# Perceiver kernel, one core: where the last values, the maximum, the NaN check and layer 3's preparations stand

## Chip, cores, metric

The kernel runs on one core of one Trainium2 chip. The metric is the device time of one execution in microseconds; 3083.25 is the median of three runs (3079.7 to 3084.26).

## What is computed

Four layers; each adds to x (128 tokens of width 256) a cross-attention over a context of 12544 tokens of width 192, then a self-attention over the 128 tokens, then a mixture of experts. The cross-attention of layers 0 to 2 has 16 heads of 16; layer 1 is its fullest form:

```python
q = (query @ Wq + bq).reshape(B, Nq, H, D).transpose(0, 2, 1, 3)
k = (key_value @ Wk + bk).reshape(B, Nkv, H, D).transpose(0, 2, 1, 3)
v = (key_value @ Wv + bv).reshape(B, Nkv, H, D).transpose(0, 2, 1, 3)
attn = jnp.einsum('bhqd,bhkd->bhqk', q, k) * scale
attn = jnp.clip(attn, -CLAMP, CLAMP)
attn = jax.nn.softmax(attn, axis=-1)
attn = jnp.where(jnp.any(jnp.isnan(attn)), jnp.asarray(1.0 / Nkv, attn.dtype), attn)
x = jnp.einsum('bhqk,bhkd->bqhd', attn, v).reshape(B, Nq, Cq)
return x @ Wo + bo
```

Layer 0 has no bias and a key mask; layer 2 has biases and neither clip nor NaN test. Layer 3 has 16 heads of 64, key and value weights with a low-rank addition (`down @ up * alpha / RANK`), and a second attention over the last four context tokens with weights of its own (`Wk_ipa`, `Wv_ipa`).

## The kernel before

A planner orders the instructions: each has a rank by its place in the program, and an engine takes the first by rank that the planner's model holds ready. So work that is written later can fill the gaps of what is written earlier: in the timeline, keys of layer 1 (tile `kv`, L102) run from 557 us on, within layer 0's self-attention, though they are written behind layer 0's experts. Each engine then runs its instructions in the order so found. `in_order` (L224) fixes the written order for some stretches.

`attend_twice_in` (L510) is the cross-attention of layers 0 to 2. For each group g of 8 heads it goes over the context's 25 blocks of 512 tokens (the last has 256) twice. In the first sweep, `highest` (L543) makes scores on TensorE (L551, with mask rows from L550 in layer 0) into one of four PSUM pairs (tile `pair`), and VectorE takes their maximum per query, head and block (`parts`, L552). Each block has four such calls: s in 0, 1 and two halves. Between them `keys.project` (L152) makes the keys and values of blocks further on, up to block 21; the keys of blocks 22 to 24 too, but not their values. `add_up` (L94) sums the context on POOL in layer 1. When the sweep is over, `project_values` (L171) makes the values of blocks 22 and 23, then of 24, on TensorE (recorded at L102), and ScalarE copies them (L136). Then come the products of `between`, if there is one, and `lowered` (L554): the maximum over blocks, negated, split into three bfloat16 parts, two transposes (L569), and a copy `m` in twice the needed width (L571). `spread` (L574) makes `less` from it (L581); layer 1 makes two `floor` tiles instead (L695). The second sweep makes the scores less the maximum (L585, L592), their exponentials (L636, L651, or L292 and L612 in layer 1), and multiplies with the values (L658).

`between` is the hook by which layer 3's preparations run there. In layer 0, `prepare_l3` (L1049) loads layer 3's key and value weights in block 3 of the first sweep, and adds the low-rank part after the sweep: four 128x512 products for the keys at the end of group 0's sweep and four for the values at the end of group 1's, each pair of products with an addition on VectorE. In layer 2, `last_tokens_l3` (L1093) loads `Wk_ipa`, makes the keys of the last four tokens after group 0's sweep, loads `Wv_ipa` into the same buffer, and makes their values after group 1's.

In layer 1, `nan_guard` (L1015) stands behind both groups: keys and queries are summed up in such a way that a NaN or infinity in them shows, and if one does, `copy_predicated` (L1012) puts the mean of the values in the place of the output `o`, before the output's projection (`project_out`, L462; its transposes are recorded at L450).

The first eight blocks' keys of the next layer (`keys.early`) are made in the self-attention and expert stages in the single PSUM pair `kv` (`early_pair`). Expert weights go through a pool of buffers of one megabyte (`large_weights`; ten in layers 0 and 2, four in 1 and 3). Their DMAs, like most, are issued by SP's queue in order; those of early context blocks by POOL's.

Of the kernel before, what the change touches and what calls it, by code (L numbers as in the profile page):

```python
# [21 lines left out]
P = 128  # L22
D = 256
# [182 lines left out]
class Net:  # L206
# [289 lines left out]
    def attend_twice(self, o, qz, keys, masked=False, clip=None, between=None):  # L496

        self.psum(ppr=4)
        with self.tc.tile_pool(name="twice", bufs=2, reuse_waits="tile") as pool:
            keys.lay(pool)
            self.attend_twice_in(pool, o, qz, keys, masked, clip, between)
        self.singles_and_early()

    def attend_twice_in(self, pool, o, qz, keys, masked, clip, between):  # L510
# [43 lines left out]
        def lowered(parts):  # L554
# [6 lines left out]
            short = self.sp.tile([P, 2, 4], BF16, tag="short", name="short")  # L561
            for j in range(2):
                nc.vector.tensor_copy(short, neg)
                nc.vector.tensor_copy(wide[:, :, :, j], short)
                self.tt(neg, neg, wide[:, :, :, j], ALU.subtract)
            nc.vector.tensor_copy(wide[:, :, :, 2], neg)
# [3 lines left out]
            m = pool.tile([P, 2, HB], BF16, tag="low", name="low", bufs=1)  # L570
            nc.vector.tensor_copy(m, bc(p[:, 0, :HB], 1, 2))  # L571
            return m.rearrange("p c n -> p (c n)")

        def spread(m, half):  # L574

            x = self.pair()
            for i in range(2):
                r = tiles[2 * half + i]
                nc.tensor.matmul(x[:, i, :HB], self.ones16[r, :], m[r, :HB], start=True, stop=True)
            less = pool.tile([P, 2, HB], F32, tag="less", name="less", bufs=1)  # L580
            nc.vector.tensor_copy(less, x[:, :, :HB])  # L581
            return less

        def less_maximum(t, x, m):
            nc.tensor.matmul(x, self.ones16[tiles[t], :], m[tiles[t], :], start=True, stop=False, skip_group_check=True)  # L585
# [30 lines left out]
        def weights(g, c, m, less, row):  # L616
# [8 lines left out]
            else:  # L625
                for j in range(2):
                    at = slice(j * HB, (j + 1) * HB)
                    k = slice((c % 4 + j) * P, (c % 4 + j + 1) * P)
                    for t in range(2):
                        r = tiles[t]  # L630
                        nc.tensor.matmul(x[t][:, at], row[r, k], m[r, at], start=j == 0, stop=False, skip_group_check=True)
# [31 lines left out]
        for g in range(2):  # L663
# [6 lines left out]
            for b in range(NSB):  # L670
# [7 lines left out]
                if between is not None and g == 0 and b == 3:  # L678
                    between[0]()

            keys.project_values(g, [NSB - 3, NSB - 2])
            keys.project_values(g, [NSB - 1])
            if between is not None:
                between[1][g][0](self.pair)
            m = lowered(parts)
            if between is not None:
                between[1][g][1]()
            floor = None
            if clip is not None:
                floor = []  # L690
                for half in range(2):
                    x = self.pair()
                    for i in range(2):
                        r = tiles[2 * half + i]
                        nc.tensor.matmul(x[:, i, :], self.ones16[r, :], m[r, :], start=True, stop=True)  # L695
                    floor.append(pool.tile([P, 2, SB], F32, tag=f"floor{half}", name="floor", bufs=1))
                    self.ts(floor[half], x, -clip, None, ALU.add)
# [38 lines left out]
            oT = pool.tile([P, 2, P], F32, tag="low" if clip is None else "oT", name="oT", bufs=1)  # L736
# [213 lines left out]
    def l0_xattn(self, x):  # L950
        nc, d = self.nc, self.d
        with self.tc.tile_pool(name="x0", bufs=2, reuse_waits="tile") as pool:
# [15 lines left out]
            with self.tc.tile_pool(name="layer3", bufs=1, reuse_waits="tile") as other:  # L968
                self.attend_twice(o, qz, keys, masked=True, between=self.prepare_l3(other))
# [15 lines left out]
    def xattn_biased(self, x, name, guarded, keys):  # L985
        nc, d = self.nc, self.d
        with self.tc.tile_pool(name=name, bufs=2, reuse_waits="tile") as pool:
# [13 lines left out]
            if guarded:  # L1001
                self.attend_twice(o, qz, keys, clip=CLAMP)
            else:
                with self.tc.tile_pool(name="layer3", bufs=1, reuse_waits="tile") as other:
                    self.attend_twice(o, qz, keys, between=self.last_tokens_l3(other))

            self.tt(o, o, bv, ALU.add)
            if guarded:
                bk = self.load_row(d[f"{name}_bk"], D)
                with self.tc.tile_pool(name="guard", bufs=1, reuse_waits="tile") as own:  # L1010
                    bad, mean = self.nan_guard(own, keys.sums, xT, wq, bq, keys.wk, keys.wv, bk, bv)
                    nc.vector.copy_predicated(o, bad.bitcast(U32), mean)  # L1012
            return self.project_out(x, o, wo, [(self.ones[:1, :], bo)])

    def nan_guard(self, pool, totals, xT, wq, bq, wk, wv, bk, bv):  # L1015
# [4 lines left out]
        sums = self.stat(2)  # L1020
        nc.vector.tensor_reduce(sums[:, 0:1], totals[:, :SB], AX.X, ALU.add)
        nc.vector.tensor_reduce(sums[:, 1:2], totals[:, SB:], AX.X, ALU.add)
        wide = pool.tile([P, 2, P], F32, tag="wide", name="wide", bufs=1)
        nc.vector.tensor_copy(wide, bc(sums, 2, P))
        many = pool.tile([1, P], F32, tag="many", name="many", bufs=1)
        nc.vector.memset(many, float(S2))
        p = self.ps()
        self.mm(p[:, :D], [(xT[:, k, :], wq[:, k, :]) for k in range(2)] + [(self.ones[:1, :], bq)])
        q = pool.tile([P, D], F32, tag="gq", name="gq", bufs=1)
        nc.vector.tensor_copy(q, p[:, :D])  # L1030
        p = self.ps()
        self.mm(p[:, :D], [(wide[:, k, :], wk[:, k, :]) for k in range(2)] + [(many, bk)])
        self.tt(q, q, p[:, :D], ALU.mult)
        self.tt(q, q, q, ALU.not_equal)
        found = self.stat(1)
        nc.vector.tensor_reduce(found, q, AX.X, ALU.max)
        p = self.ps()
        self.mm(p[:, :1], [(self.ones, found)])
# [794 lines left out]
```

## Time and profile before

One execution was profiled: 3080.96 us, of which the profile's span is 3079.3 us; its mean granted TensorE clock was 0.966. Stages, read from the timeline, with the busy time in each:

| Stage | from, to (us) | PE | DVE | ACT |
|---|---|---|---|---|
| Layer 0: self-attention and experts | 556 to 685 | 99.2 | 59.1 | 31.2 |
| Layer 1: cross-attention, NaN check | 685 to 1224 | 525.1 | 474.6 | 256.7 |
| Layer 1: output, self-attention | 1224 to 1290 | 55.2 | 44.2 | 22.5 |
| Layer 2: cross-attention | 1361 to 1877 | 506.0 | 364.0 | 243.8 |
| Layer 2: self-attention | 1877 to 1914 | 31.5 | 22.6 | 12.5 |
| Layer 2: experts | 1914 to 1977 | 51.4 | 29.1 | 17.8 |

The six first sweeps of layers 0 to 2 end (last L552) at 163.3, 431.3, 814.1, 1081.6, 1489.7 and 1751.4 us. The busy time of a matmul is a modelled duration and overlaps with its neighbours', so a stage that shows PE busy may still have room in it. In the lines of the profile, `L102` is a helper for keys and values, `L278` and `L289` to `L298` are helpers for matmuls and VectorE operations of many places: there the tile's name says what is meant. A matmul in float32 appears as two records.

### The profile page before, as it was taken

The page shows a single profiled execution, that of the slowest core. Times are in us where ns is not written, and L with a number is a line of the kernel's source. Part 1 is how long each engine was busy: PE and PEld are TensorE (multiplying, and loading weights), DVE is VectorE, ACT ScalarE, POOL GpSimd, SP SyncE. Part 2 cuts the span into 40 slices and gives each one's busy share as a digit, 9 for nine tenths or more (in the row PEclk, how much of TensorE's full clock was granted, in tenths as well). Part 3 has the DMA queues.
Part 4 walks back from the last instruction along what each step waited for, and adds up shares of the span by engine and source line. Part 5 has one row for each costly group of instructions (what it writes and reads, how often), then busy time and mean ns, then how long its engine had stood idle before and what let it go on. Part 6 is the DMA issues. An engine that isn't in the chain of part 4 may idle for free.

```text
span 3079.3 us, 78420 instructions
## 1 busy us (share of the span) xinstructions
PE 2923.5 (95%) x34877; PEld 2212.8 (72%) x34877; DVE 2249.7 (73%) x2887; ACT 1428.3 (46%) x1673; POOL 456.7 (15%) x501
## 2 busy tenths in 40 slices
PE   8999999879999999899999998899999999999979
PEld 5667667535576576675676576489889889889858
DVE  6876877638997897769658755477777777777854
ACT  1167128411383176311482295356556555656521
POOL 6666577212000000120000001000000000000000
PEclk9989999989999998999899999899999999999979
DMA  4200210552002101442102106332322222222436
GB/s 128 60 18 22 70 47 4 190 203 60 27 3 58 55 18 39 135 155 57 31 9 72 50 3 216 109 93 80 85 85 82 85 80 85 85 82 85 123 113 205
DMA packets 166858, 246.96 MB, mean 80 GB/s; under 512 B 21261, under 2 KB 108431, under 8 KB 166520
## 3 DMA queue, kind: packets, MB, share of 16 engines
q1 hardware_dynamic: 160200, 227.67, 24.3%
q0 software_dynamic: 6208, 14.27, 1.5%
q8 instruction: 274, 4.49, 0.6%
q14 instruction: 64, 0.52, 0.1%
q10 hardware_dynamic: 112, 0.01, 0.0%
HBM read 241.75 MB, written 0.13 MB: 79 GB/s over the span
## 4 chain that ended last, share of the span: by engine, by line
PE 79%; DVE 14%; issue 2%; ACT 2%; DMA 2%; POOL 1%; SPq 0%; DVEq 0%; ACTq 0%; POOLq 0%
PE pair L102 20%; PE pair L551 10%; PE acc L658 8%; PE v L102 7%; PE sc L790 6%; PE acc L832 5%; PE pair L592 4%; PE ps L278 4%; PE one L592 4%; DVE parts L552 3%; DVE e L292 2%; PE kv L102 2%; PE acc L278 2%; PE pair L585 2%; PE ps L1624 1%
## 5 line engine op out<-in xcount | busy, mean ns | idle before, releaser
L552 DVE TENSOR_REDUCE parts<-pair 128x2 f32<-128x1024 f32 x600 | 679.3, 1197 | 108.2 <-PE pair L551 108.0
L102 PE MATMUL pair<-ctxA,wk 128*128 128x256 f32 x1236 | 329.7, 400 | 1.4 <-ACT kT L193 1.1
L102 PEld LDWEIGHTS pair<-ctxA,wk 128*128 128x128 f32 x1236 | 217.5, 190 | 140.8 <-DVE parts L552 95.2
L551 PE MATMUL pair<-kT,qz 32*128 32x512 f32 (+1 forms) x1632 | 278.6, 617 | 9.1 <-DVE parts L552 8.9
L289 DVE TENSOR_TENSOR top<-top,kept 128x1024 f32<-128x1024 f32 (+2 forms) x145 | 169.1, 1169 | 133.8 <-ACT kept L792 132.5
L792 ACT COPY kept<-sc 128x1024 f32<-128x1024 f32 (+1 forms) x135 | 136.3, 1010 | 261.1 <-PE sc L790 261.1
L636 ACT ACTIVATE e<-pair 128x1024 f32<-128x1024 f32 x196 | 200.7, 1024 | 82.5 <-PE pair L592 62.1
L292 DVE SCALAR_TENSOR_TENSOR e<-pair,floor 128x1024 f32<-128x1024 f32 x196 | 230.5, 1219 | 6.5 <-PE pair L592 0.4
L612 ACT ACTIVATE e<-e 128x1024 f32<-128x1024 f32 x196 | 206.6, 1057 | 33.7 <-DVE e L292 26.5
L592 PE MATMUL pair<-qz,kT 32*128 32x256 f32 x2112 | 219.0, 374 | 0.0
L536 POOL TENSOR_SCALAR row<-mask 128x512 bf16<-128x512 uint8 (+1 forms) x100 | 189.6, 1896 | 173.7 <-PE pair L551 102.5
L658 PE MATMUL acc<-e,v 128*17 128x128 f32 x6336 | 211.4, 274 | 3.1 <-ACT e L651 2.2
L132 ACT ACTIVATE kT<-pair,bk 128x512 f32<-128x512 f32 (+1 forms) x68 | 45.9, 674 | 348.2 <-PE pair L102 348.2
L292 DVE SCALAR_TENSOR_TENSOR e<-one,maskcol,less 128x256 f32<-128x256 f32 x392 | 162.6, 477 | 58.4 <-PE one L592 41.7
L651 ACT ACTIVATE e<-e 128x1024 f32<-128x1024 f32 x196 | 205.1, 1048 | 0.0
L658 PEld LDWEIGHTS acc<-e,v 128*17 128x17 f32 x6336 | 155.8, 97 | 67.9 <-ACT e L651 45.6
L790 PE MATMUL sc<-qz,kT 64*128 64x128 f32 x2816 | 197.8, 279 | 0.0
L102 PEld LDWEIGHTS v<-wv,ctxA 128*128 128x128 f32 x1568 | 189.8, 192 | 6.4 <-issue 1.7
L102 PE MATMUL v<-wv,ctxA 128*128 128x128 f32 x1568 | 193.1, 276 | 0.0
L289 DVE TENSOR_TENSOR e<-one,less 128x512 f32<-128x512 f32 x196 | 126.4, 686 | 88.8 <-PE pair L592 87.6
L102 PE MATMUL pair<-ctxB,wk 64*128 64x256 f32 x1236 | 188.9, 399 | 0.0
L790 PEld LDWEIGHTS sc<-qz,kT 64*128 64x128 f32 x2816 | 171.6, 187 | 13.0 <-issue 1.3
(439 smaller groups left out, 5495.2 us busy)
## 6 DMA issues: line engine op xcount, KB each, us to landing
ctxA<-in_ctxA SPq DMA_DIRECT2D x324, 256.0 KB
ctxB<-in_ctxB SPq DMA_DIRECT2D x339, 128.0 KB
w<-in_L_ffn_W SPq DMA_DIRECT2D x32, 1024.0 KB
ctxA<-in_ctxA POOLq DMA_DIRECT2D x36, 256.0 KB, 3.1
w<-in_L_ffn_w_gateT SPq DMA_DIRECT2D x8, 1024.0 KB
wu<-in_L_ffn_w_upT SPq DMA_DIRECT2D x8, 1024.0 KB
w<-in_L_ffn_w_downT SPq DMA_DIRECT2D x8, 1024.0 KB
w<-in_L_ffn_w1T SPq DMA_DIRECT2D x8, 1024.0 KB
```

Source lines behind the costliest of these rows:

```text
L102: self.nc.tensor.matmul(out, a, b, start=start and not low, stop=low == 1, skip_group_check=True)
L289: self.nc.vector.tensor_tensor(out, a, b, op)
L292: self.nc.vector.scalar_tensor_tensor(out, a, s, b, op0, op1, **kw)
L536: nc.gpsimd.tensor_scalar(row[:, :n], to[:, :n], 0.0, 1.0, ALU.is_gt, ALU.subtract)
L551: nc.tensor.matmul(x[:, i, :n], qz[r, g, s, :], keys.kT(b)[r, :n], start=not masked, stop=True)
L552: nc.vector.tensor_reduce(parts[:, s, 2 * half : 2 * half + 2, b], x[:, :, :n], AX.X, ALU.max)
L592: nc.tensor.matmul(at, keys.kT(c // 4)[tiles[t], k], q, start=start, stop=True, skip_group_check=True)
L612: nc.scalar.activation(to, to, AF.Exp)
L636: nc.scalar.activation(to, pair, AF.Exp)
L651: nc.scalar.activation(to, to, AF.Exp)
L658: nc.tensor.matmul(acc[32 * t : 32 * t + 17, half, :], v[:, c % 4 + j, 4 * half + t, :], es[half][:, t // 2, j, t % 2, :], start=c + j + h ...
L790: nc.tensor.matmul(x[:, t, c : c + P], kT[r, c : c + P], qz[r, g, :], start=True, stop=True)
```

## The change

- The values of blocks 22, 23 and 24 are made inside the first sweep: after the four score calls of block 22, after the first two of block 23, and after its last two.
- `lowered` follows the sweep directly. It writes its parts with ScalarE copies and reads the short form back from its own tile; `m` is kept once in bfloat16 and read twice through a broadcast, so its copy is 256 wide and no longer 512. `less` is copied by ScalarE. In layer 1 `floor` is written by four instructions and no longer two.
- The hook is split: `load` (layer 0, block 3) and `guard` (layer 1, group 0). The low-rank additions are written after layer 0's self-attention, in the early pair (`add_low_l3`). The last tokens' loads and products are written at the end of layer 2's self-attention, with both weights in the buffers of the expert weights.
- The NaN check's sums, products and test run around the maximum of layer 1's group 0; behind the attention only the flag's copy and `copy_predicated` are left.

```diff
@@ lowered, spread, less_maximum
-            short = self.sp.tile([P, 2, 4], BF16, tag="short", name="short")
             for j in range(2):
+                short = self.sp.tile([P, 2, 4], BF16, tag="short", name="short")
                 nc.vector.tensor_copy(short, neg)
-                nc.vector.tensor_copy(wide[:, :, :, j], short)
-                self.tt(neg, neg, wide[:, :, :, j], ALU.subtract)
-            nc.vector.tensor_copy(wide[:, :, :, 2], neg)
+                nc.scalar.copy(wide[:, :, :, j], short)
+                self.tt(wide[:, :, :, 2] if j else neg, neg, short, ALU.subtract)
...
-            m = pool.tile([P, 2, HB], BF16, tag="low", name="low", bufs=1)
-            nc.vector.tensor_copy(m, bc(p[:, 0, :HB], 1, 2))
-            return m.rearrange("p c n -> p (c n)")
+            m = pool.tile([P, 2 * HB], BF16, tag="low", name="low", bufs=1)
+            nc.vector.tensor_copy(m[:, :HB], p[:, 0, :HB])
+            return m[:, :HB]
...
-            nc.vector.tensor_copy(less, x[:, :, :HB])
+            nc.scalar.copy(less, x[:, :, :HB])
...
-            nc.tensor.matmul(x, self.ones16[tiles[t], :], m[tiles[t], :], start=True, stop=False, skip_group_check=True)
+            by_chunk = x.rearrange("p (j n) -> p j n", j=2)
+            nc.tensor.matmul(by_chunk, self.ones16[tiles[t], :], bc(m[tiles[t], :], 1, 2), start=True, stop=False, skip_group_check=True)
@@ the first sweep
-                if between is not None and g == 0 and b == 3:
-                    between[0]()
-
-            keys.project_values(g, [NSB - 3, NSB - 2])
-            keys.project_values(g, [NSB - 1])
-            if between is not None:
-                between[1][g][0](self.pair)
+
+                    if NSB - 3 <= 2 * b + s - NSB + 2 < NSB:
+                        keys.project_values(g, [2 * b + s - NSB + 2])
+                if load is not None and g == 0 and b == 3:
+                    load()
+                if b == NSB - 1 and guard is not None and g == 0:
+                    guard[0]()
+            if guard is not None and g == 0:
+                guard[1](self.pair)
             m = lowered(parts)
-            if between is not None:
-                between[1][g][1]()
+            if guard is not None and g == 0:
+                guard[2]()
@@ floor
-                    self.ts(floor[half], x, -clip, None, ALU.add)
+                    twofold = floor[half].rearrange("p i (j n) -> p i j n", j=2)
+                    for i in range(2):
+                        self.ts(twofold[:, i], bc(x[:, i, :HB], 1, 2), -clip, None, ALU.add)
@@ xattn_biased, layer 1
+                    parts, bad, mean = self.nan_guard(own, keys.sums, xT, wq, bq, keys.wk, keys.wv, t[:1, :D], bv)
+                    self.attend_twice(o, qz, keys, clip=CLAMP, guard=parts)
+
+                    self.tt(o, o, bv, ALU.add)
+                    nc.vector.copy_predicated(o, bad().bitcast(U32), mean)
@@ nan_guard: the three parts of guard
+        def sums():
+            s = self.stat(2)
+            nc.vector.tensor_reduce(s[:, 0:1], totals[:, :SB], AX.X, ALU.add)
+            nc.vector.tensor_reduce(s[:, 1:2], totals[:, SB:], AX.X, ALU.add)
+            nc.vector.tensor_copy(wide, bc(s, 2, P))
+            nc.gpsimd.memset(many, float(S2))
+
+        def products(bank_pair):
+            p = bank_pair()
+            self.mm(p[:, 0, :D], [(xT[:, k, :], wq[:, k, :]) for k in range(2)] + [(self.ones[:1, :], bq)])
+            self.mm(p[:, 1, :D], [(wide[:, k, :], wk[:, k, :]) for k in range(2)] + [(many, bk)])
+            made.append(p)
+            p = bank_pair()
+            self.mm(p[:, 0, :D], [(wide[:, k, :], wv[:, k, :]) for k in range(2)])
+            made.append(p)
+
+        def kept():
+            p, last = made
+            q = pool.tile([P, D], F32, tag="wide", name="gq")
+            nc.vector.tensor_copy(q, p[:, 0, :D])
+            self.tt(q, q, p[:, 1, :D], ALU.mult)
+            self.tt(q, q, q, ALU.not_equal)
+            nc.vector.tensor_reduce(found, q, AX.X, ALU.max)
+            self.stt(mean, last[:, 0, :D], 1.0 / S2, bv, ALU.mult, ALU.add)
+            self.mm(last[:, 1, :1], [(self.ones, found)])
+            self.ts(found, last[:, 1, :1], 0.0, None, ALU.is_gt)
@@ layer 3's low-rank part, after layer 0's self-attention
+    def add_low_l3(self):
+
+        for i, w in enumerate(self.w3):
+            at = slice(i * RANK, (i + 1) * RANK)
+            for c in range(2):
+                p = self.early_pair()
+                for h in range(2):
+                    self.mm(p[:, h, :], [(self.downs[at, c * P : (c + 1) * P], self.ups[at, h * 512 : (h + 1) * 512])])
+                part = w[:, c, :].rearrange("p (h e) -> p h e", h=2)
+                self.stt(part, p, self.rate[:, i + 1 : i + 2], part, ALU.mult, ALU.add)
@@ last_tokens_l3, called at the end of l2_attn
+        wk = self.load_kv(d["L3_xattn_Wk_ipa"], dims, "wi")
+        wv = self.load_kv(d["L3_xattn_Wv_ipa"], dims, "wi")
...
+        p = self.early_pair()
+        for g in range(8):
+            self.mm(p[:, 0, g * n : (g + 1) * n], [(wk[rows[k], k, g * P : (g + 1) * P], given[k]) for k in range(2)])
...
+        p = self.early_pair()
+        for h in range(2):
+            c = slice(h * 512, (h + 1) * 512)
+            self.mm(p[: H * n, h, :], [(many[rows[k], k].rearrange("p h k -> p (h k)"), wv[rows[k], k, c]) for k in range(2)])
@@ run
+                if layer == 0:
+                    self.add_low_l3()
+                    low3.__exit__(None, None, None)
```

## The prediction

> **What bounds the kernel now.** I read the page first, then the chain of waits, then the timeline around the six places that the change touches, and last the busy time by stretches.
>
> ```profile
> PE   8999999879999999899999998899999999999979
> ...
> L552 DVE TENSOR_REDUCE parts<-pair 128x2 f32<-128x1024 f32 x600 | 679.3, 1197 | 108.2 <-PE pair L551 108.0
> ...
> L551 PE MATMUL pair<-kT,qz 32*128 32x512 f32 (+1 forms) x1632 | 278.6, 617 | 9.1 <-DVE parts L552 8.9
> ```
>
> TensorE (PE) is called busy for 95%, but its ends are modelled; what counts is which wait ends last in a stage. Layers 0 to 2 make six maximum passes (two groups of heads each). Each ends alike; the chain of waits around the last one (layer 2, second group) shows it, start and length in us:
>
> ```profile
> 1737.61 10.28 DVE parts L552 x9
> 1747.89 0.04 issue
> 1747.93 2.35 PE pair L551 x8
> 1750.29 6.41 PE pair L102 x40
> 1756.69 4.02 PE pair L278 x8
> 1760.71 0.02 issue
> 1760.73 0.68 DVE vi L289
> ```
>
> VectorE (DVE) sets the pace of the last scores. Then TensorE alone works: 6.41 us of values of the last three blocks (L102), 4.02 us of layer 3's products (L278). Only then come the transposes of the maximum, though VectorE has had it ready since 1753.2 (timeline). The second place is the end of layer 1:
>
> ```profile
> 1212.84 0.24 DVE L1024 COPY wide<-st 128x256 f32<-128x256 f32 x1
> ...
> 1217.22 1.19 PE L278 MATMUL ps<-row,many 1*128 1x256 f32 x2 [0.27 <-DMA row<-in_L_xattn_bk]
> ...
> 1223.77 0.45 DVE L1012 COPY_PREDICATED o<-bad,mean 128x256 f32<-128x256 uint32 x1
> ...
> 1224.27 0.69 PE L450 MATMUL tr<-ident,o 128*128 128x128 f32 x2 [1.00 <-DVE o L1012]
> ```
>
> The NaN check is a serial chain from 1212.84 to 1224.22 with nothing of weight beside it. Third, the stages to which work goes (layer 0's and layer 2's self-attention, with what follows), by stretches; columns are stretch, length, then busy time and count of PE, its weight loads, DVE, ACT, POOL, clock, DMA share, GB/s:
>
> ```profile
> 555.00:612.00 57.00, 48.04 (x274) 31.11 (x266) 35.77 (x130) 19.10 (x30) 17.22 (x22) 0.96 0.70 251
> 612.00:690.00 78.00, 57.18 (x507) 31.12 (x506) 25.09 (x78) 12.79 (x27) 7.71 (x30) 0.81 0.57 201
> ...
> 1205.00:1235.00 30.00, 24.89 (x221) 16.84 (x216) 12.41 (x34) 9.01 (x14) 1.07 (x2) 0.72 0.42 131
> ...
> 1875.00:1935.00 60.00, 49.58 (x233) 33.01 (x232) 33.91 (x95) 17.89 (x25) 15.50 (x31) 0.92 0.85 289
> ```
>
> TensorE has 9, 21 and 10 us free in the first, second and fourth, not in one piece.
>
> **What the skill says.** "TensorE: Matmul & The Clock Gate", section on the HAM clock gate: an idle window of some 3.4 us halves the clock. Partly agreed: the clock was 0.72 from 1205 to 1235, where gaps are short but many. "VectorE: DVE Perf Modes", section on the TRN2 errata: small operands pay a fixed cost each; agreed: 128x8 casts take 0.17 us and follow each other every 0.21. "ScalarE: Activation LUTs", section What ACT_TABLE_LOAD costs: 1.28 us [...]placed right before the activation; the trace shows the same 1.28 us (at 169.47, hidden).
>
> **Part 1: values between the scores.** A pass's values are three bundles, from the timeline 4.75 us for two full blocks and 1.35 for the half one at full clock, so 2.4, 2.4, 1.3, sum 6.1. They now follow the last score of block 22, the first half and the second half of block 23. In layer 2, second group, TensorE finishes block 22's last scores at 1742.8, when VectorE has only about 1.2 us left of block 22: it is barely ahead. VectorE then has four full maxima (1.16 us each, block 23) and four halves (0.68): 7.35 us. TensorE needs 0.57 us for a full score pair and 0.3 for a half. Step by step: 1742.8 + 2.4 + 0.6 = 1745.8, where VectorE wanted it at 1744.05 (1.8 lost); two maxima to 1748.2, but the next score waits for the second bundle until 1749.4 (1.2 lost). The third fits. So 3.0 us of 6.1 show and 3.1 are hidden. The same sum elsewhere: layer 0, with mask matmuls in every score (0.66 us each), 3.4 twice; layer 1 1.8 and 3.0; layer 2 2.75 and 3.0. Sum of losses 17.35. Unknown: the order into which the instructions fall and the four PSUM pairs; bounds 10 (all but 1.7 us a pass hidden) and 36.6 (nothing hidden).
>
> **Part 2: the maximum follows directly.** From the end of the last maximum to the first scores of the weights (in layer 1, to the first clipped score on VectorE, which bounds there), by the timeline: 14.2, 11.1 (layer 0), 8.85, 9.85 (layer 1), 10.95, 10.7 (layer 2), sum 65.65. After: reduction 0.36, two casts and two subtractions at 0.21 each give 1.2; the last ScalarE copy adds about 0.2 (nearest row: 128x16 activation, 0.21; bounds 0.15 and 0.5); transposes at 1.4; their result 0.5 later, as at 818.71 to 819.19; the cast, now 256 wide, 0.42 (L737's row) for 0.68; scores at 2.4. In layer 0 they wait for the copy of "less" as before (1.2 more, moved to an idle ScalarE at 0.58): 3.7. Layer 1's second group adds the clip (0.2), the matmul and four floor instructions of 128x512 (0.68 each, row L296, for two of 1.17): 5.85. First group: part 3. The exp table load, now close ahead of the first exponential, has 2 us of scores beside it; cost nothing, up to 1.3 in two passes if not.
>
> **Part 3: the NaN check.** In the first group of layer 1 it adds two reductions, a broadcast copy, eight matmuls (3.6 us at full clock), five VectorE instructions near 0.42 and a matmul on their result. Behind that last matmul stands the floor's matmul, so VectorE's floor waits for VectorE's own check. I take sums 1.35, chain 1.6, products to 4.0, transposes by 4.5, maximum 5.4, then rest of the check and floor: first clipped score 9.85 after, against 8.85; bounds 8 and 12. So the six intervals become 3.7 + 3.7 + 9.85 + 5.85 + 2.4 + 2.4 = 27.9, a gain of 37.75. At the layer's end the interval 1213.28 (o ready) to 1224.27 shrinks to adding bv 0.42, the predicated copy 0.45 and small change: gain 9.8, of which I take 9.3, since the copy of the flag (0.29) may stand there. Next layer's key weights (SP's queue waited for them at 1216.98 and 1223.30, behind which wqkv stood until 1224.25) are free earlier, so wqkv comes earlier too. What is late next: the output projection and norm, unchanged.
>
> **Part 4: layer 3's preparations.** Off the passes go 5.37 + 3.70 (low rank, layer 0) and 5.2 + 4.07 us (last tokens, layer 2) of TensorE, 18.3; their absence is already in part 2. They arrive: in layer 0, four pairs of matmuls (7.4 us at full clock) and four 128x1024 additions on VectorE (1.28 each, 5.1), each holding the only early pair until added. They go ahead of layer 1's first eight key blocks (557 to 623 now). VectorE has gaps of 3.6 and 3.7 us at 563 and 569; later its work is dense to 603. I take 3 us: one or two additions in the dense part, plus a megabyte of context loads pushed into the weight-bound part after 633. Bounds 0 and 9. In layer 2, 32 small matmuls (5.0), 8 wide ones (4.1), 1.5 us of VectorE and two POOL copies; SP's queue gets six weight DMAs (2 MB, about 7 us at 289 GB/s) ahead of the expert weights, in two of their ten buffers. Expert weights were in by about 1911 and used from 1933.6, so the DMAs are covered, if the two buffers come free by then. POOL gets a mask and copies ahead of its context DMAs. TensorE's 10 us free there take most, but fillers delay the VectorE chain and early keys spill into the experts: 4 us, bounds 0 and 9.3. SP's loads at the start of layer 2 (1359) go: nothing, they were hidden.
>
> **Sum.** 37.75 - 17.35 + 9.3 - 3 - 4 = 22.7 us. Against the profiled execution (3080.96 us, span 3079.3) this is 3058.3; the median of the runs, 3083.25, lies 2.3 above it, so 3060.5 on that footing. I predict 3060.
>
> **The rivals.**
> - Nothing moved costs anything (gaps take parts 1 and 4 well: losses 10, moved work 0): 37.75 - 10 + 9.3 = 37, 3046. For it: the idle shares above. Against: TensorE barely ahead of VectorE at 1742.8.
> - The moved products cost their full length (18.3), the rest as summed: 37.75 - 17.35 + 9.3 - 18.3 = 11.4, 3072. For it: TensorE 83% busy in both stages, in-order fillers.
> - Slower: TensorE is the bound wherever work lands. In the tails of the passes all values show (36.6) and in the self-attention stages all products (18.3): 54.9 against gains of 47: 8 us slower, 3091. For it: 95% busy. Against: 0.4 to 0.8 us waits for L552 between scores in the tail, and the weight-bound experts of layer 0. It decides from the point where over 86% (47 of 54.9) of the displaced work shows.
> - The change doesn't do what it says: the values end up behind the scores anyway. Then the products leave the passes (18.3), 7 come back and the check's 9.3 go: about 3062, the same answer for another reason.
>
> **How the numbers follow.** Forecast 0.5, the free case 0.2, full-cost products 0.15, order unchanged 0.05, slower 0.1. A difference under 0.2% (6 us) can't be told from none. The forecast's own range is 3052 to 3069. With the free case's and the full-cost case's spread, 3044 to 3078. The slower case (0.1) and the tails beyond leave 0.2 outside. Faster 0.83: forecast, free, order unchanged and 0.08 of the full-cost case; same 0.08: its other 0.07 and 0.01 of the slower case; slower 0.09.
>
> **What would show it.** In the trace of after: L102 values among L551 in the tail, VectorE with two gaps of 1 to 2 us there; transposes about 1.4 us after the last maximum; no check between o and its transposes at layer 1's end; early keys of layer 1 ending near 637. Wrong if those keys hold up the experts, if the first group of layer 1 starts its weights more than 12 us after its last maximum, or if layer 2's experts start over 5 us later after the pass than now.

## The result, and the profile after

The changed kernel takes 3068.43 us, the median of 15 runs (3062.48 to 3082.34); the kernel before, run beside it, 3083.29 (3078.3 to 3089.08, 15 runs). The ratio is 0.9956, with a 95% interval of 0.9944 to 0.9969: 15 us faster. The profiled execution went from 3080.96 to 3066.55 us, its span from 3079.3 to 3064.8, so the two traces compared here differ by as much as the medians. The page of after (busy row of TensorE, then the two groups shown of before):

```profile
PE   8999999879999999899999998899999999999979
...
L552 DVE TENSOR_REDUCE parts<-pair 128x2 f32<-128x1024 f32 x600 | 680.1, 1197 | 118.1 <-PE pair L551 116.8
...
L551 PE MATMUL pair<-kT,qz 32*128 32x512 f32 (+1 forms) x1632 | 265.8, 609 | 5.2 <-DVE parts L552 5.1
```

VectorE now waits 118.1 us ahead of the maxima where it waited 108.2: the values among the last scores cost 10 us. What the change brings shows in the chain of waits at the end of layer 2's second pass (start, length in us, what):

```profile
1726.43 4.76 DVE parts L552 x6
1731.19 0.02 issue
1731.21 0.37 DVE st L558
...
1732.22 0.21 ACT wide L564
1732.43 0.11 issue
1732.54 0.42 PE pair L568 x2
...
1733.46 0.39 PE pair L578 x2
```

The 6.41 us of values and 4.02 us of products behind the last maximum are gone, and the transposes start 1.36 us after it. At the end of layer 1 the check's chain has gone too. The timeline of VectorE in after (start, length, line, operation, and in brackets the idle time and who ended it):

```profile
1206.83 0.45 DVE L1012 COPY_PREDICATED o<-bad,mean 128x256 f32<-128x256 uint32 x1
...
1211.04 0.18 DVE L434 BATCH_NORM_AGGREGATE mv<-bn 128x2 f32<-128x6 f32 x1
1215.17 0.17 DVE L289 TENSOR_TENSOR dot<-q,k 128x16 f32<-128x16 f32 x1 [3.95 <-DMA k<-in_L_attn_lambda_k]
...
1215.47 0.14 DVE L296 TENSOR_SCALAR st<-mv 128x1 f32<-128x1 f32 x1
```

Here a new wait stands in the old one's place: a small product for lambda (a factor that layer 1's self-attention computes from four short vectors) waits for an 8 KB row, and the layernorm's next step is queued behind it. The trace of before has the wait for that row too; there it lay within the check's chain and cost nothing:

```profile
1221.27 0.17 DVE L289 TENSOR_TENSOR dot<-q,k 128x16 f32<-128x16 f32 x1 [1.42 <-DMA k<-in_L_attn_lambda_k]
```

The stretches between fixed events of both traces (last maximum of a pass, first exponential or clipped score, sums of x) give the whole difference, in us, gain positive:

| Part | predicted | measured |
|---|---|---|
| six gaps between last maximum and weights (74.7 to 36.1) | 37.75 | 38.6 |
| weights behind the gaps (layer 0, first group: 113.9 to 118.6) | 0 | -4.8 |
| six tails of the first sweeps (whole sweeps; their last eight maxima alone: -10.9) | -17.35 | -11.1 |
| NaN check: end of layer 1 +11.6, self-attention behind it -3.2, way to layer 2 -1.9 | 9.3 | 6.5 |
| layer 0: self-attention 45.7 to 53.8, experts 74.7 to 67.3, projection | -3 | -1.8 |
| layer 2: self-attention 37.1 to 48.1 | -4 | -11.1 |
| rest (layer 3's cross-attention 2.2) | 0 | -2.0 |
| sum | 22.7 | 14.4 |

### The profile page after: what moved, and what is told of

Its sections match the earlier page's. It is cut to its first block, busy times and chain, and to the rows that moved or that the text cites. A ratio compares the mean times of both kernels' runs of the same rounds, so it can differ in the third digit from the quotient of the medians.

```text
span 3064.8 us, 78395 instructions
## 1 busy us (share of the span) xinstructions
PE 2910.1 (95%) x34877; PEld 2204.4 (72%) x34877; DVE 2239.5 (73%) x2867; ACT 1433.2 (47%) x1689; POOL 458.1 (15%) x502
## 4 chain that ended last, share of the span: by engine, by line
PE 82%; DVE 10%; issue 3%; ACT 2%; DMA 2%; POOL 1%; SPq 0%; DVEq 0%; POOLq 0%; ACTq 0%
PE pair L102 20%; PE pair L551 10%; PE v L102 8%; PE acc L658 8%; PE sc L794 6%; PE acc L836 6%; PE pair L592 4%; PE ps L278 4%; PE one L592 4%; DVE parts L552 2%; DVE e L292 2%; PE kv L102 2%; PE acc L278 2%; PE pair L585 2%; PE pair L550 1%
## 5 line engine op out<-in xcount | busy, mean ns | idle before, releaser
L552 DVE TENSOR_REDUCE parts<-pair 128x2 f32<-128x1024 f32 x600 | 680.1, 1197 | 118.1 <-PE pair L551 116.8
L551 PE MATMUL pair<-kT,qz 32*128 32x512 f32 (+1 forms) x1632 | 265.8, 609 | 5.2 <-DVE parts L552 5.1
L612 ACT ACTIVATE e<-e 128x1024 f32<-128x1024 f32 x196 | 207.2, 1057 | 43.6 <-DVE e L292 36.1
```

Of the source, the lines that this page charges most:

```text
L551: nc.tensor.matmul(x[:, i, :n], qz[r, g, s, :], keys.kT(b)[r, :n], start=not masked, stop=True)
L552: nc.vector.tensor_reduce(parts[:, s, 2 * half : 2 * half + 2, b], x[:, :, :n], AX.X, ALU.max)
L612: nc.scalar.activation(to, to, AF.Exp)
```

## The experiments

Two questions were open: why layer 2's self-attention cost 11 us and not 4, and what each part of the change is worth. All twelve kernels are edits of the changed one. "Stretch" is the time between the sums of x before and after a stage, from the profiled execution. Medians are set beside the changed kernel's 3068.4; ratios are to the kernel before, run beside them, whose median lay between 3081.2 and 3083.6 us, so that 2 us between two medians can come from that alone. Where a ratio's interval overlaps with the changed kernel's (0.9944 to 0.9969), as most do, the reading rests on the stretches, and each of these comes from one execution.

**Products behind the turned queries and keys.** In the trace of after, layer 2's small products stand at the head of TensorE's queue (timeline of TensorE):

```profile
1849.92 0.56 PE L278 MATMUL kv<-lastA,wi 128*128 128x4 f32 x2 [0.49 <-DMA wi<-in_L_xattn_Wk_ipa]
1851.70 0.69 PE L450 MATMUL tr<-ident,xn 128*128 128x128 f32 x2 [1.22 <-DVE xn L298]
1852.78 0.59 PE L278 MATMUL kv<-lastB,wi 64*128 64x4 f32 x2 [0.40 <-DMA wi<-in_L_xattn_Wk_ipa]
...
1859.50 0.59 PE L278 MATMUL kv<-lastA,wi 128*128 128x4 f32 x2
1859.95 2.05 PE L278 MATMUL ps<-wq,xT 128*128 128x256 f32 x4
```

So the query projection waits from 1852.8 to 1859.95. The edit:

```diff
+            turned = [i for i in nc.cur_bb.bb.instructions if i.engine == mybir.EngineType.PE][-1]
...
+            n = len(nc.cur_bb.bb.instructions)
             self.last_tokens_l3(pool)
+            info = mybir.DependencyInfo(mybir.DependencyClass.NoSync, mybir.DependencyReason.DATA)
+            for ins in nc.cur_bb.bb.instructions[n:]:
+                if ins.engine == mybir.EngineType.PE:
+                    self.tc.add_manual_dep(ins, turned.name, info, reason="in order")
```

> The changed kernel, but TensorE may start layer 2's last-token products only behind the turned queries and keys of layer 2's self-attention. Theory (the products stand at the head of TensorE's queue while their weights are still landing): the stretch between the residual sums before and after that self-attention goes from 48.1 us to 39-41 (it was 37.1 before the change), and the kernel is 7-9 us faster than the changed one, near 3060. Rival (the products are simply more work on that path, wherever they stand): the stretch stays at 45 us or more and the time within 2 us of the changed kernel's.

Measured: 3074.45 us (3065.60 to 3081.28, 18 runs), ratio 0.9975 [0.9966, 0.9983]; the stretch is 52.3 us. My theory fell: out of the head of the queue, the products still cost as much. The stretches of this profile pointed elsewhere. Layer 0's self-attention, which the edit doesn't touch, took 59.4 us here and 53.8 in the changed kernel. The figures by stretches, for the kernel before, the changed one and this one, over layer 0's self-attention (length, busy time and count of PE, PEld, DVE, ACT, POOL, clock, DMA share, GB/s):

```profile
560.50:606.17 45.67, 40.03 (x196) 24.60 (x192) 32.57 (x119) 12.95 (x21) 14.40 (x19) 1.00 0.81 291
```

```profile
552.20:606.01 53.81, 48.44 (x182) 26.78 (x182) 35.66 (x123) 13.28 (x20) 12.59 (x16) 0.87 0.65 235
```

```profile
551.00:610.38 59.38, 54.64 (x182) 28.95 (x182) 34.44 (x122) 13.40 (x20) 12.53 (x16) 0.77 0.60 213
```

Clock 1.00, 0.87, 0.77: the loss is in TensorE's clock. In all fourteen traces the clock is either full or half, so the mean tells how long it was half: 0, 13.7 and 27.3 us. Less half of that, the three stretches are 45.7, 47.0 and 45.7 us. This corrected length (an estimate, since half clock costs nothing while TensorE waits) is the same in all fourteen profiles, 44.8 to 47.2 us.

**Early keys back in their place.** In the kernel before, early keys of the next layer fill TensorE's pauses in self-attention (its timeline shows `kv<-ctxA,wk` ahead of `ps<-wq,xT` at 1879.90). They use the single PSUM pair `kv`. The moved products were given that pair too, and ahead of them: in after, layer 1's early values start at 577.8, not 558.3. Two kernels give the early keys their place back; the diffs are cut to layer 0, and layer 2's products are moved in the same way. The first puts the moved products into self-attention's own banks:

```diff
-                p = self.early_pair()
                 for h in range(2):
-                    self.mm(p[:, h, :], [(self.downs[at, c * P : (c + 1) * P], self.ups[at, h * 512 : (h + 1) * 512])])
+                    p = self.ps()
+                    self.mm(p, [(self.downs[at, c * P : (c + 1) * P], self.ups[at, h * 512 : (h + 1) * 512])])
```

> The changed kernel, but the moved products of layer 0 and layer 2 use a bank of self-attention's pool instead of the single buffer that the next layer's early keys and values need too. Theory (the moved products took that buffer, so that the early keys and values of the next layer, which filled TensorE's idle moments before the change, came 20 us later and the clock fell to half): early keys and values stand in self-attention again, granted clock there 0.95 or more, self-attention of layer 0 at 45-48 us (53.8 in the changed kernel, 45.7 before) and of layer 2 at 37-40 (48.1, 37.1 before), experts behind layer 0's self-attention longer by up to 7 us since their weights set the pace; total 8-12 us faster than the changed kernel. Rival (the products themselves take that time on TensorE): both stretches within 2 us of the changed kernel's.

The second keeps the pair and writes the early keys ahead of the products and the experts:

```diff
                 x = among[layer](x)
+                if layer < 3:
+                    made = next_keys[layer]()
                 if layer == 0:
                     self.add_low_l3()
...
-            if by_place:
-                made = next_keys[layer]()
```

> The changed kernel, but the early keys and values of the next layer are given out ahead of the moved products and of the experts, in the same single buffer. Theory as for the kernel with the other bank: self-attention of layer 0 at 45-48 us and of layer 2 at 37-40, at a granted clock of 0.95 or more; the products come among the experts, whose stretch grows by 0-5 us. Rival (whichever comes second in that buffer costs the same): what self-attention gains the experts lose, total within 3 us of the changed kernel.

Measured: 3088.47 us (3084.92 to 3099.62, 16 runs), ratio 1.0020 [1.0011, 1.0030], and 3090.68 us (3084.36 to 3100.53, 16 runs), ratio 1.0028 [1.0017, 1.0038]: both slower than the kernel before. The first half of the theory held: layer 0's self-attention 46.0 and 46.6, layer 2's 36.3 and 36.6. The second half fell: the experts paid. Layer 2's experts, 60.4 us in the changed kernel, took 86.0 and 81.0; layer 0's 83.0 and 88.7 instead of 67.3. Layer 2's self-attention and experts, other bank:

```profile
1857.81:1894.06 36.25, 30.92 (x156) 21.64 (x153) 22.65 (x48) 12.41 (x17) 10.18 (x19) 0.97 1.05 353
1894.06:1980.03 85.97, 80.06 (x478) 36.79 (x477) 28.86 (x92) 17.61 (x35) 5.84 (x15) 0.66 0.48 154
```

The products now stand in TensorE's queue ahead of the norm and the router of the experts, run at half clock, and their weights hold two of the ten buffers until then. From the profiles, for layer 2's self-attention (length, time at half clock, length less half of that):

| Kernel | length | half clock | corrected |
|---|---|---|---|
| before | 37.1 | 3.2 | 35.4 |
| layer 2 undone | 37.1 | 3.3 | 35.4 |
| other bank | 36.3 | 2.4 | 35.1 |
| early keys first | 36.6 | 3.1 | 35.1 |
| changed | 48.1 | 17.4 | 39.4 |
| products behind | 52.3 | 25.0 | 39.8 |
| filler products (below) | 53.7 | 29.8 | 38.8 |

Over all fourteen profiles the corrected length is 38.8 to 40.0 us with the products in that stage and 35.1 to 35.6 without. So the products are worth about 4 us of work there; the rest, 7 us by this estimate, is clock. In layer 0 the five profiles whose self-attention has the early keys and not the products show 0 to 3.4 us at half clock, the nine others 13.7 to 32.1, though these nine run the same code there. No kernel had both in self-attention, so the experiments don't tell apart whether the missing early keys or the products let the clock fall. For layer 2 the trace of after tells a part of it. From 1853 to 1859.7 us TensorE runs nothing but last-token products of four columns, without a pause, and stays at the half clock to which it had fallen at 1849.5 (two stretches, columns as above):

```profile
1854.00:1856.00 2.00, 2.00 (x9) 1.93 (x9) 0.00 (x0) 0.00 (x0) 0.00 (x0) 0.50 1.07 307
1856.00:1858.00 2.00, 2.00 (x9) 1.93 (x9) 0.00 (x0) 0.00 (x0) 0.00 (x0) 0.50 0.23 53
```

Such products don't bring the clock back, however busy they look; the last section counts it.

**Each part undone alone.**

```diff
@@ layer 2: products at the two gaps, as before the change
-            self.last_tokens_l3(pool)
+                    self.attend_twice(o, qz, keys, between=self.last_tokens_l3(other))
@@ NaN check behind the attention, as before
-                    self.attend_twice(o, qz, keys, clip=CLAMP, guard=parts)
+                self.attend_twice(o, qz, keys, clip=CLAMP)
@@ layer 0: low-rank products at the two gaps, as before
-                    self.add_low_l3()
+                self.attend_twice(o, qz, keys, masked=True, between=self.prepare_l3(other))
@@ values behind the sweep, as before
-                    if NSB - 3 <= 2 * b + s - NSB + 2 < NSB:
-                        keys.project_values(g, [2 * b + s - NSB + 2])
+            keys.project_values(g, [NSB - 3, NSB - 2])
+            keys.project_values(g, [NSB - 1])
```

(Four kernels, one edit each; the diffs are cut to the lines that decide.)

> The changed kernel, but the last-token products of layer 3 stand at layer 2's two gaps again, as before the change. Expected: self-attention of layer 2 at 37-38 us instead of 48.1, each of the two gaps 4.0-4.8 us longer; net 1-3 us faster than the changed kernel. Rival (the move was worth it, since the gaps cost more than self-attention gives back): 2 us or more slower.

Measured: 3065.95 us (3064.51 to 3068.40, 4 runs), ratio 0.9942 [0.9921, 0.9962]. Self-attention 37.05 us; the gaps +7.2 and +0.6, not 4 to 5 each. Net 3.4 us less by these stretches; but the weights behind the two gaps took 2.9 us more and 0.6 less, which leaves 1.0. It can't be told from the changed kernel: no gain of the move shows.

> The changed kernel, but the NaN check stands at the end of layer 1's cross-attention again. Expected: first gap of layer 1 shorter by 4-5 us, its end longer by 10-12 us, the self-attention behind it shorter by 3-4 us because the rows of lambda are there by then; net 2-5 us slower than the changed kernel. Rival (9 us slower, as my sum had it): self-attention keeps its 60.4 us.

Measured: 3073.45 us (3066.26 to 3080.18, 13 runs), ratio 0.9967 [0.9955, 0.9979]. End of layer 1 +10.1, self-attention -2.7, first gap only -1.7: net 5.7 us slower, close to what the accounts of the change have (6.5). The intervals overlap.

> The changed kernel, but the low-rank products of layer 3's weights stand at layer 0's two gaps again. Expected: gaps longer by 7 and 5 us, self-attention of layer 0 shorter by 8 us, the experts behind it longer by 7 us because their weights set the pace; less half clock behind the gaps (3-6 us); net 3-10 us slower than the changed kernel. Rival (the move only shifts time): within 2 us.

Measured: 3073.27 us (3064.50 to 3078.32, 10 runs), ratio 0.9963 [0.9950, 0.9977]. Gaps +2.7 and +2.5, self-attention -6.6, experts +6.3. Two numbers of mine were off (7 and 5 for the gaps); the total expectation was met by the median, but the profile ends later mainly in layer 1's self-attention (66.6 us with 24.2 at half clock; 60.4 with 8.5 in the changed kernel), which the edit doesn't touch. With the weights behind the two gaps, which are 2.1 and 4.8 us shorter, the layer's own stretches come to 2.0 us less: the move only shifts time.

> The changed kernel, but the values of the last three blocks stand behind the sweep again, ahead of the maximum's transposes; the rest of the change stays. Theory (the chain behind the last maximum waits for TensorE): the transposes start 4-5 us after the last maximum instead of 1.4, each tail loses 1.5-2.3 us, TensorE stays at full clock through the gap, net 5-11 us slower than the changed kernel. Rival (the tail is bound by TensorE, so that values cost the same wherever they stand): gap and tail cancel, within 2 us.

Measured: 3063.02 us (3061.53 to 3067.21, 4 runs), ratio 0.9936 [0.9911, 0.9961]. Not slower. The transposes do wait, 4.2 us from the last maximum, as VectorE's timeline in the last pass shows (3.50 us idle for TensorE):

```profile
1730.78 0.17 DVE L289 TENSOR_TENSOR wide<-st,short 128x8 f32<-128x8 f32 x1
1734.46 0.42 DVE L570 CAST low<-pair 128x256 bf16<-128x256 f32 x1 [3.50 <-PE pair L568]
```

But from the last maximum to the weights the six gaps grew by 13.8 us in all (5.5 of them in layer 1's first pass, where the check's products stand behind the values too), and the last eight maxima of the six sweeps took 10.9 us less, so by these stretches the place of the values is worth 2.9 us. The weights of layer 0 then ran 9.9 us faster (112.9 and 109.0 us for 118.6 and 113.1): TensorE had come busy through the gap and ran at full clock, where the changed kernel has 13.7 us at half clock from each of the two gaps on. In this comparison, moving the values by itself lost more in clock than it gained.

**The values last, and a filler.** In after, TensorE does nothing from the last score to the transposes, 3.7 us in layer 0's first pass (3.0 in layer 2's second), and then runs at half clock from 166.7 to 180.4. The stretch of the first weights, in after:

```profile
170.55:180.38 9.83, 9.65 (x104) 6.24 (x102) 4.97 (x12) 4.96 (x5) 3.49 (x4) 0.50 0.00 0
```

One kernel fills the gap with work that is due there anyway, the values of the last two blocks; those of block 22 move one block later:

```diff
-                    if NSB - 3 <= 2 * b + s - NSB + 2 < NSB:
-                        keys.project_values(g, [2 * b + s - NSB + 2])
+                    if 2 * b + s == 2 * NSB - 3:
+                        keys.project_values(g, [NSB - 3])
...
+            keys.project_values(g, [NSB - 2])
+            keys.project_values(g, [NSB - 1])
             if guard is not None and g == 0:
```

> The changed kernel, but the values of the last two blocks stand right behind the last scores instead of among them; those of the third last stay among them. Theory (TensorE has 3 us or more with nothing to do between the last score and the transposes, which hides 2.1 us of values and keeps its clock up): the transposes still start 1.4 us after the last maximum, each of the six tails loses 1.0-1.3 us, and the half clock after the gap (the first 10 us of the weights of layer 0's first pass) does not show; 7-15 us faster than the changed kernel. Rival (they delay the transposes, or their evictions on ScalarE delay the copies of the maximum): the gap grows by what the tails lose, 0.6-1.2 us per pass, total within 3 us.

Measured: 3058.14 us (3055.32 to 3062.42, 4 runs), ratio 0.9931 [0.9915, 0.9948]; each of the four runs is below the lowest of the changed kernel's fifteen, and the two intervals just overlap. The tails are as before the change (1.3 to 2.3 us less each; 1.0 to 1.3 were expected), the gaps nearly as in after (-0.9 to +1.1), and in layer 0's first pass TensorE comes through the gap at full clock. The weights behind it take 113.9 us (118.6 in after); those of the second pass, 113.4, gain nothing (113.1). TensorE's timeline, then the stretch of the first weights:

```profile
160.30 0.64 PE L551 MATMUL pair<-kT,qz 32*128 32x256 f32 x8
160.87 1.16 PE L102 MATMUL pair<-wv,ctxA 128*128 128x128 f32 x8
161.96 0.72 PE L102 MATMUL pair<-wv,ctxB 64*128 64x128 f32 x8
162.60 0.71 PE L102 MATMUL pair<-wv,ctxA 128*128 128x128 f32 x4
163.24 0.71 PE L102 MATMUL pair<-wv,ctxB 64*128 64x128 f32 x4
164.34 0.41 PE L568 MATMUL pair<-ident,wide 128*128 128x128 f32 x2 [0.39 <-DVE wide L289]
```

```profile
167.48:177.30 9.82, 9.21 (x202) 6.70 (x202) 8.12 (x20) 8.48 (x9) 6.70 (x7) 1.00 0.02 4
```

In the same 9.8 us TensorE has 202 matmul records for 104. The values, 3.1 us from 160.87 to 163.95 and not the 2.1 of the expectation, fit into the time in which otherwise only VectorE's and ScalarE's chain runs.

The other kernel fills it with work for nobody:

```diff
             p = self.pair()
+            for i in range(3):
+                nc.tensor.matmul(p[:, 1, :], qz[:, g, 0, :], keys.kT(NSB - 3), start=True, stop=True)
```

> The changed kernel with three products of 128x512 that nobody reads, between the last score and the transposes of the maximum: TensorE is busy there, and all else stays. Theory (the idle 3-3.7 us there let the clock drop to half): no stretch of half clock behind the gap, the first exponentials of layer 0's first pass 2.2 us apart instead of 3.1, 4.1 and 3.5, so 3-5 us less in each pass of layer 0 and up to 10 us in all. Rival (the half clock comes from a throttle that does not know of the gap, or the wide spacing from the masks): spacing and time as in the changed kernel, or slower where the products delay the transposes.

Measured: 3082.77 us (3063.36 to 3092.04, 12 runs), ratio 0.9999 [0.9983, 1.0016]: the expectation missed. The gaps shrank by 0.4 to 0.9 us and the weights of layer 2 by 1.0 and 0.6, but in layer 0 the clock still fell, at 167.8, and the self-attentions of this profile had 32.1, 16.7 and 29.8 us at half clock (13.7, 8.5 and 17.4 in after). Half of the differences is 19.5 us, and the profiled span is 18.2 us longer. In layer 0's first pass the filler ends at 164.9, too early: the clock goes by windows of a fixed grid (last section), and of the one ahead of the fall, 164.4 to 167.8, TensorE is busy for 0.55. In after that window is idle throughout; with the values last the two windows there are busy for 0.73 and 0.79, and the clock stays. Keeping one gap busy does not keep the stages behind it busy either; why these fell so often to half clock is not settled beyond what the last section shows.

**Lambda behind the layernorm.**

```diff
-            l1, l2 = self.dot_exp(pool, "q1", "k1"), self.dot_exp(pool, "q2", "k2")
+            vs = [self.all_rows(d[f"L1_attn_lambda_{k}"], 16, k, pool) for k in ("q1", "k1", "q2", "k2")]
+            xT = self.normed(x)
...
+            l1, l2 = self.dot_exp(pool, *vs[:2]), self.dot_exp(pool, *vs[2:])
...
-            xT = self.normed(x)
```

> The changed kernel, but VectorE computes layer 1's lambda only behind the first layernorm of the self-attention, not ahead of it. Theory (the two small products wait in VectorE's queue for their 8 KB rows and hold up the layernorm): the stretch between the residual sums before and after layer 1's self-attention goes from 60.4 us to 56-57, the total 3-4 us down. Rival (the weights of queries and keys land no earlier than those rows, so that the layernorm's result would wait for them): the stretch stays within 1 us of 60.4.

Measured: 3065.24 us (3061.23 to 3074.74, 5 runs), ratio 0.9960 [0.9940, 0.9980]; the stretch is 59.8 us, as the rival has it. In detail neither is right: the copy of the turned layernorm starts 3.9 us after the sum of x, where it took 8.2, but the stage has 14.5 us at half clock for 8.5. Corrected for that it is 3.5 us shorter. Inconclusive in the time.

**Do the gains add?**

> Two edits together: the values of the last two blocks behind the last scores, and the last-token products of layer 3 at layer 2's two gaps again. Expected if the gains add: tails of the six passes as before the change, self-attention of layer 2 at 37 us, first gap of layer 2 longer by 7 us, second by 1-3; median 3052-3057, 2-5 us faster than the values alone (3058). Rival (values and products together fill the gap beyond what it hides): both gaps of layer 2 longer by 5 us or more and no gain over the values alone.

> As the kernel with two edits, and the low-rank products of layer 0 at layer 0's two gaps again too. Expected if the gains add: layer 0's gaps longer by 2.5-5 us each, its self-attention at 46-48 us at a granted clock of 0.95 or more, the experts behind it at 73-75; 0-4 us faster than with layer 2's part alone, near 3052. Rival (layer 0's move is the better place, since the experts hide it): 3 us or more slower than with layer 2's part alone.

Measured: 3067.54 us (3064.90 to 3072.02, 5 runs), ratio 0.9956 [0.9942, 0.9970], and 3063.98 us (3059.39 to 3064.84, 4 runs), ratio 0.9938 [0.9919, 0.9956]. They don't. Against the values alone, layer 2's products lengthen its gaps by 7.1 and 5.2 us and its experts by 4.3, for 9.4 less in self-attention: the rival. Against two edits, layer 0's products lengthen its gaps by 4.2 and 5.1 us and its experts by 6.6, and self-attention gives 13.0 back; the median is 3.6 us lower, within the 0 to 4 expected, but these stretches show no gain and the intervals overlap. The lowest median is that of the changed kernel with the values of the last two blocks last, 3058.14 us; its interval overlaps with those of the kernel with all three edits and of the one with all values behind the sweep.

## Why the prediction was right, and where its size was off

- The forecast (3060, own range 3052 to 3069) and its direction held; the median came out 8 us above the forecast and 0.6 us inside the range. That it stayed inside is partly luck: tails that were put 6.3 us too dear made up for about half of what was missed on the clock (4.8 and some 7 us). By the total alone, the rival in which the moved products cost their full length (3072) lies nearer. And one of the prediction's signs of being wrong, layer 2's experts starting over 5 us later after the pass, came true if it is counted from the end of the cross-attention (11 us later; 3 from the last maximum).
- Part 2 held: 37.75 us predicted, 38.6 measured to the first exponential or clipped score, 38.3 to the prediction's own events (65.6 to 27.3); 2.4 us to the first product of the last pass was 2.28. In layer 1's first pass the total was met (9.85 predicted, 9.79 measured), but not the way there: the transposes came at 2.64 us, not by 4.5, since the check's products began ahead of the last maximum.
- Part 1's tails were too dear by 6.3 us (17.35 against 11.1). The two waits that my walk had at 1.8 and 1.2 us in the last pass were 1.25 and 0.45. What the part was worth against values behind the sweep the sum didn't ask: there the gap grows by 2.3 us a pass on average, not by the 6.1 us of their length, since a part of them (2.6 of 5.7 us in the last pass) runs while VectorE still takes its last maximum and makes the parts.
- What I had not seen: an emptied gap lets TensorE's clock fall. I quoted the clock gate for the end of layer 1 and did not apply it to the gap that part 2 makes; 4.8 us. The kernel with the values last shows it.
- Part 3: 9.3 us at the layer's end was 11.6, but 3.2 came back in the self-attention behind it. "What is late next: the output projection and norm, unchanged" was the step that failed: late next was an 8 KB row for lambda, for which VectorE waits 3.95 us. Undoing the part alone showed 5.7 us in its stretches. That the row is worth 3 us isn't shown by the time: without its wait the stage took 59.8 us for 60.4, with more half clock.
- Part 4, layer 2: 4 us, bounds 0 and 9.3, measured 11.1, outside these bounds. As work the term was right (39.4 less 35.4 us, corrected for half clock: 4.0). Put at nothing was the clock: 7 us of the 11 by the same estimate. "Early keys spill into the experts" was in the prediction, without the thought that what fills TensorE's pauses can also hold its clock up. The four-column products don't, as the traces show; that the early keys would have is likely, but no run shows it apart.
- Part 4, layer 0: 3 us predicted, 1.8 measured, as the difference of two larger numbers: self-attention +8.1 (its corrected length +1.3), experts -7.3.
- Of the rivals, the full length of the moved products (18.3 us) did not come; that they cost where they land, wherever that is, did: in gaps, self-attention or experts layer 2's cost 7.7, 11.1 and over 20 us.

## What to carry to other kernels

Before a serial chain is cleared of work, ask what the bulk engine then does meanwhile: work that is due and fits into the chain's length belongs there, as 3.1 us of values in 3.7 us here. When work is moved, look at what it pushes out of a shared buffer as well as at its own length, and at whether it holds the clock up as what it pushes out did. And compare stages at equal clock before a microsecond is put down to an edit.

## What the runs showed of the hardware

TensorE's clock changes only at points of a fixed grid of 3.41 us; in each of the fourteen profiles all its changes differ by multiples of that. "TensorE: Matmul & The Clock Gate", section "What's actually happening", says that the window is free-running and 3413 ns long, which these traces agree with, and that half clock comes after an idle window. Here idle is not needed: of 377 falls to half clock, eight followed a window that was busy for under a tenth. I counted, over all fourteen profiles, how much of a window the matmul records cover (modelled ends) and the clock of the next:

| Window | busy under 0.5 | 0.5 to 0.65 | 0.65 to 0.8 | 0.8 to 0.97 | over 0.97 |
|---|---|---|---|---|---|
| at full clock, next one half | 209 of 221 | 98 of 296 | 29 of 346 | 25 of 808 | 16 of 10023 |
| at half clock, next one half | 109 of 109 | 60 of 60 | 68 of 70 | 69 of 96 | 177 of 511 |

A window that is half busy can be enough to lose the clock, and one that is nearly full was needed in most cases to have it back. Between, a window keeps the clock that it has: busy for 0.65 to 0.8, full clock fell in 29 of 346 cases and half clock stayed in 68 of 70.

Busy by the records is not all that counts. Twenty windows, at least one in each profile, are covered throughout by layer 2's last-token products of four columns and hold nothing else; all twenty were followed by half clock, also the one that began at full clock.

The clock goes with the spread of one kernel's runs, 20 us in the changed kernel: the mean clock was 0.967 to 0.970 in its runs of 3062 to 3067 us and 0.962 in those of 3079 and 3082. As an estimate, 0.969 less 0.962, of 3070 us, is 21 us of full clock. That the place on the grid at which a run starts decides it was not tried.
